# Where the attention starts, where the lists stand and how many expert units are open in a one-core attention and mixture-of-experts block

## The chip, the core and the metric

The kernel runs on one core of a Trainium2 chip, as one program with one launch. The time is device microseconds of that core. Each engine of a core executes its own instructions in order: TensorE (PE in the profile, its weight loads PEld) multiplies, VectorE (DVE), ScalarE (ACT) and GpSimd (POOL) work on elements, and SyncE (SP), ACT and POOL issue transfers. Engines wait for each other through semaphores.

## The reference

The input x is 2 x 1024 x 256. Every row is normalised (mean and variance over 256) to xn, and the output is x + attention(xn) + ffn(xn).

```python
# attention: xn seen as tokens of 16 channels, on a grid of 256 x 64
qkv = tok @ qkv_w                                    # 16 -> 48
x1 = branch(q[:8], k[:8], v[:8], 1 x 8 windows)      # softmax(q k / sqrt(8)) v + 3x3 convolution of v
x2 = branch(q[8:], k[8:], v[8:], 8 x 1 windows)
att = concat(x1, x2) @ proj_w + proj_b
tok = tok + layernorm(att) * ln_w + ln_b
# ffn: 16 experts of 176 hidden units, the best 6 of a row, and one shared expert of 352 units
topk = 6 of the experts in the 2 best of 4 groups, by sigmoid(xn @ gate.T) + bias
out = sum over the 6 of weight * (silu(xn @ g_e.T) * (xn @ u_e.T)) @ d_e.T
out = out + (silu(xn @ sg.T) * (xn @ su.T)) @ sd.T
```

## The kernel before

**Stages.** The kernel normalises the 2048 rows, finds each row's six experts on DVE, and sorts the rows by their set of experts, so that the 16 tiles of 128 sorted rows each have six experts in common for most of their rows. While that is computed, PE works on the shared expert, whose steps `shared_steps` are let in by `meanwhile(until)`. A step `products(k, m)` makes the two products of 512 rows, `gated` multiplies silu of one by the other (ACT L283, DVE L284), and `down` makes the output of 128 rows (PE L290), which ACT writes to `ysum` (L291) and POOL adds to the output in DRAM (L293).

**Units.** Then comes a loop over 55 units of two experts each (L1124). A unit is `six` (two of the six experts of a sorted tile, three units a tile) or `extra` (two lists of 128 rows that have some other expert). Lists are made by `lists_begun` and `lists_ended` while the first units run; the seven extra units stand behind tiles `FIRST` to `FIRST + 6`. Per expert, `up` makes the products for gate and up (PE L867), ACT takes silu (L869, to `sg`), and DVE multiplies (L870, to `hms`): this is called the gating product below. Per unit, `hidden` transposes the two experts' products (PE L881, ACT copy L883), and `finished` makes the output (PE L893 or L901). `hms` has two buffers: `hidden` of unit u - 1 and `finished` of unit u - 2 follow the two `up` of unit u. For an extra unit, POOL gathers rows (L994), PE transposes them (L1001), and ACT copies them (L1003) ahead of `up`. The output of each tile or list goes to `ysum` (L1047, L1054), from which POOL adds it to the output by an indirect DMA (`to_out`, L1008). Two additions to the output are never open at once: each waits until the one before has landed.

**The walk.** The attention is a list of steps, here called the walk (`attention_steps`), that is laid between the units. It has four blocks (batch b, half h of the channels). A block gathers its rows (ACT L670), projects them in eight steps (`project`: PE L675, four ACT copies L677 to L680 each), and then works on DVE alone but for one Exp (ACT L700): products L688, sums L692, maximum and difference L698, L699, weighted values L709, L714, totals L703, L704, division L722. Then PE transposes the result (`transposed`, L729) and ACT copies it to `oT` (L731). Behind the fourth block come the projection of the output and the convolution (`attended`, PE L781) and the normalisation (`normed`, L791 to L806), and eight DMAs that add the attention to the output (L1079).

**Pace.** The walk is paced by a written cost of every step on DVE and on PE: `walked` lets steps in as long as the DVE cost so far is under `pace` times the PE cost so far.

```python
of_slot = {"six": (0.5, 2.0), "extra": (0.8, 2.5)}
END = 84
pace = (whole[0] - LEAD - END * of_slot["six"][0] / of_slot["six"][1]) / (whole[1] - END)
```

`END` is the PE cost that is to be left when the walk ends. The first part of the walk, the gathering and the eight projections of block 0, is let in ahead of the last steps of the shared expert:

```python
sorted_tile(0)
walked(FIRST_ROWS - LEAD)
sorted_tile(1)
meanwhile(100)
walked()
```

**Order.** A scheduler orders the instructions of each engine from the program, so neighbours in the program can change places in the built order.

## Time and profile before

| | |
|---|---|
| median of three runs | 449.19 us (448.36 to 451.4) |
| the profiled execution's own time | 448.94 us |
| its span, first to last instruction | 447.2 us |
| mean granted TensorE clock | 0.978 |
| PE busy | 393.4 us, 88% |
| DVE busy | 293.0 us, 66% |
| ACT busy | 215.6 us, 48% |
| POOL busy | 187.8 us, 42% |
| additions by indirect DMA (L1008) | 30, mean 1701 ns of POOL each |

Busy time is the union of an engine's instructions. The ends of matmuls are modelled, so a PE that is busy throughout is not a PE at its peak. A granted clock of 0.50 is half speed. In the lists of groups and of the timeline a row has line, engine, operation, output and inputs; in brackets stands how long the engine was idle before, and what it waited for.

### The profile page before, as it was taken

The page shows a single profiled execution, that of the slowest core. Times are in us where ns is not written, and L with a number is a line of the kernel's source. Part 1 is how long each engine was busy: PE and PEld are TensorE (multiplying, and loading weights), DVE is VectorE, ACT ScalarE, POOL GpSimd, SP SyncE. Part 2 cuts the span into 40 slices and gives each one's busy share as a digit, 9 for nine tenths or more (in the row PEclk, how much of TensorE's full clock was granted, in tenths as well). Part 3 has the DMA queues.
Part 4 walks back from the last instruction along what each step waited for, and adds up shares of the span by engine and source line. Part 5 has one row for each costly group of instructions (what it writes and reads, how often), then busy time and mean ns, then how long its engine had stood idle before and what let it go on. Part 6 is the DMA issues. An engine that isn't in the chain of part 4 may idle for free. (4 is left out here: it accounts for less than half of the span.)

```text
span 447.2 us, 6291 instructions
## 1 busy us (share of the span) xinstructions
PE 393.4 (88%) x1668; PEld 247.4 (55%) x1669; DVE 293.0 (66%) x515; ACT 215.6 (48%) x535; POOL 187.8 (42%) x207
## 2 busy tenths in 40 slices
PE   0999999997887979898898899999899999999970
PEld 0445565655554646665565476566655555666750
DVE  4627958679997948979779599398992333322110
ACT  2955247462472355372462452735335777843220
POOL 7400000220556145886504235324542778791431
PEclk9999999998999999999999699999999999999995
DMA  8999942320423110121012133202331129347222
GB/s 236 314 290 328 272 170 42 48 82 12 86 70 85 22 20 22 33 38 39 22 24 45 52 60 65 44 20 63 85 58 38 22 65 141 74 70 101 44 33 24
DMA packets 40178, 37.56 MB, mean 84 GB/s; under 512 B 5300, under 2 KB 37616, under 8 KB 40112
## 3 DMA queue, kind: packets, MB, share of 16 engines
q0 software_dynamic: 11616, 13.52, 18.4%
q1 hardware_dynamic: 27472, 22.59, 16.6%
q10 hardware_dynamic: 1056, 1.05, 0.7%
q8 instruction: 15, 0.25, 0.2%
q14 instruction: 19, 0.16, 0.1%
HBM read 27.70 MB, written 12.45 MB: 90 GB/s over the span
## 5 line engine op out<-in xcount | busy, mean ns | idle before, releaser
L867 PE MATMUL pr_u<-w1s,xsT 128*128 x384 | 128.3, 468 | 2.7 <-DVE hms L870 2.1
L867 PEld LDWEIGHTS pr_u<-w1s,xsT 128*128 128x128 f32 x384 | 69.9, 190 | 39.3 <-issue 7.1
L1008 POOL DMA_INDIRECT out_dram<-ysum,lists x30 | 51.0, 1701 | 88.5 <-ACT ysum L1047 38.0
L869 ACT ACTIVATE sg<-pr_u 128x176 f32<-128x176 f32 x110 | 34.6, 317 | 83.1 <-PE pr_u L867 73.6
L870 DVE SCALAR_TENSOR_TENSOR hms<-sg,w,pr_u 128x176 f32<-128x176 f32 x96 | 37.4, 392 | 49.1 <-ACT sg L869 46.6
L688 DVE TENSOR_TENSOR pr<-qk 128x2048 f32<-128x2048 f32 x16 | 36.6, 2288 | 15.8 <-ACT qk L677 15.3
L709 DVE TENSOR_TENSOR pv<-s,v 128x2048 f32<-128x2048 f32 x16 | 36.6, 2286 | 4.2 <-ACT s L700 4.2
L692 DVE TENSOR_REDUCE s<-pr 128x256 f32<-128x2048 f32 x16 | 36.5, 2281 | 0.1
L714 DVE TENSOR_REDUCE o<-pv 128x256 f32<-128x2048 f32 x16 | 36.4, 2272 | 0.0
L293 POOL DMA_DIRECT2D out_dram<-ysum x4 | 3.7, 914 | 76.1 <-ACT ysum L291 76.1
L881 PEld LDWEIGHTS ph<-ident,hms 128*128 128x128 f32 x165 | 21.4, 141 | 19.8 <-issue 8.0
L994 POOL DMA_INDIRECT xg<-xw_d,lists x14 | 21.2, 1512 | 26.2 <-DVE hms L870 23.7
L881 PE MATMUL ph<-ident,hms 128*128 128x128 f32 x165 | 29.5, 276 | 2.2 <-DVE hms L870 1.7
L969 POOL TENSOR_SCALAR ysum<-row_h,spot 128x128 f16<-128x128 f16 x26 | 21.3, 825 | 23.4 <-PE rows_of L960 17.0
L827 POOL DMA_INDIRECT xg<-xw_d,lists x16 | 21.6, 1353 | 18.7 <-PE px__1007 L835 6.5
L893 PE MATMUL pr_y<-w2a,hT 128*128 x96 | 28.7, 380 | 0.0
L893 PE MATMUL pr_y<-w2b,hT 112*128 x96 | 28.7, 379 | 0.0
L893 PE MATMUL pr_y<-wts,hT 128*128 128x256 f32 x96 | 28.5, 379 | 0.0
L290 PE MATMUL py<-room 128*128 128x256 f32 x96 | 25.3, 402 | 2.5 <-DVE room L284 2.5
L883 ACT COPY hT<-ph 128x384 f32<-128x384 f32 x55 | 26.3, 479 | 1.9 <-PE ph L881 1.2
L675 PE MATMUL pq<-wq,rows 128*128 128x384 f32 x64 | 24.8, 503 | 2.5 <-ACT oT L731 1.4
L867 PE MATMUL pr_u<-w1s,xd 128*128 x56 | 21.8, 518 | 5.1 <-ACT xd L1003 4.6
(403 smaller groups left out, 703.6 us busy)
## 6 DMA issues: line engine op xcount, KB each, us to landing
w1s<-in_w_dram SPq DMA_DIRECT2D x22, 256.0 KB
wts<-in_w_dram SPq DMA_DIRECT2D x55, 64.0 KB
wts<-in_w_dram SPq DMA_DIRECT2D x55, 48.0 KB
xw_d<-xx SPq DMA_DIRECT2D x4, 544.0 KB
w2a<-in_w_dram SPq DMA_DIRECT2D x4, 512.0 KB
out_dram<-ysum POOLq DMA_DIRECT2D x4, 512.0 KB, 6.8
xr<-xw_d POOLq DMA_DIRECT2D x4, 512.0 KB
out_dram<-att POOLq DMA_DIRECT2D x8, 256.0 KB, 4.1
```

The costliest lines, as they stand in the source:

```text
L290: nc.tensor.matmul(py, lhsT=hms[k, m][:, P * c : P * c + P], rhs=w2h[:, m], start=(m == 0), stop=(m == 2))
L688: nc.vector.tensor_tensor(pr, q_.unsqueeze(3).to_broadcast(full), k_.unsqueeze(2).to_broadcast(full), ALU.mult)
L692: nc.vector.tensor_reduce(out=s[:, n : n + NW], in_=held.pop(n), axis=AX.X, op=ALU.add)
L709: nc.vector.tensor_tensor(pr, s[:, n : n + NW].unsqueeze(3).to_broadcast(full), v[:, br, m : m + NW].unsqueeze(2).to_broadcast(full), ALU. ...
L714: nc.vector.tensor_reduce(out=o[:, n : n + NW], in_=held.pop(n), axis=AX.X, op=ALU.add)
L867: nc.tensor.matmul(pu, lhsT=lhs[:, h, :], rhs=w1s[:, :, h, bass.ds(e * I, I)], start=(h == 0), stop=(h == 1))
L869: nc.scalar.activation(sg, pu[:, 0, :], AF.Silu)
L870: nc.vector.scalar_tensor_tensor(hm[:, 0:I], sg, w, pu[:, 1, :], op0=ALU.mult, op1=ALU.mult)
L881: nc.tensor.transpose(ph[:, s, :], units[:, P * s : P * s + P], ident)
L883: nc.scalar.copy(hT, ph)
L893: nc.tensor.matmul(py, lhsT=l_, rhs=r_, start=start and n == 0, stop=stop and n == 2)
L1008: nc.gpsimd.indirect_dma_start(out=out_rows, out_offset=bass.IndirectOffsetOnAxis(ap=index, axis=0), in_=ys, in_offset=None, bounds_check= ...
```

## The change

It has four parts.

1. `walked(FIRST_ROWS - LEAD)` is removed: the walk's first steps now follow `meanwhile(100)`, which lets in all that is left of the shared expert.
2. `FIRST` goes from 7 to 8: the first extra unit is unit 27 and not 24, and the last is unit 51 and not 48.
3. `END` goes from 84 to 96, so `pace` from 1.143 to 1.199.
4. From unit `DEEP` = 27 on, three units are open: `hms` has a third buffer (in `ysum`), `hidden` of unit u - 2 follows the first `up` of unit u, and `finished` of unit u - 2 the second; for an extra unit, the second list's `finished` is moved half a unit further. Every fourth `up` from there on takes its PSUM tile from the tag `y1`, so four such tiles are open in place of three. `sg` has three buffers in place of two. To make room, `RING` goes from 4 to 3 (tiles of `ysum` that wait to be added to the output, three for tiles of rows and three for lists), lists use only the PSUM tag `y0`, and some constants of the attention's preparation share a tile of `ysum`.

```diff
-FIRST = 7
-RING = 4
+FIRST = 8
+RING = 3
...
-    hms = work.tile([P, 2, 2, P + HALF], F32, name="hms")
+    hms2 = work.tile([P, 2, 2, P + HALF], F32, name="hms")
+    hms = [hms2[:, 0], hms2[:, 1], ysum[:, 6:8].rearrange("p n d -> p (n d)")[:, 0 : 2 * (P + HALF)].rearrange(
+        "p (e u) -> p e u", e=2)]
...
     def up(hm, lhs, e, w):
-        pu = ps_u.tile([P, 2, I], F32, tag="u", name="pr_u")
+        ups.append(hm)
+        fourth = len(ups) > 48 and len(ups) % 4 == 0
+        pu = (ps_t if fourth else ps_u).tile([P, 2 * I], F32, tag="y1" if fourth else "u", name="pr_u",
+                                             padded_shape=[P, TB]).rearrange("p (a i) -> p a i", a=2)
...
-        sg = work.tile([P, I], F32, tag="sg", name="sg", bufs=2)
+        sg = work.tile([P, I], F32, tag="sg", name="sg", bufs=3)
...
-    def finished(what, hT, wt, e):
+    def finished(what, hT, wt, e, q):
         kind, n, k = what
+        if kind == "six" and q == 0:
+            return
...
         else:
-            for q in range(2):
-                py = sum_tile(1 - q)
-                down_one(py, hT, wt, e[q], q)
-                ys = ysum[:, RING + (n + q) % 4, :]
-                nc.scalar.copy(ys, py)
-                done_.append((ys, lists[:, n + q : n + q + 1]))
+            py = sum_tile(0)
+            down_one(py, hT, wt, e[q], q)
+            ys = ysum[:, RING + (n + q) % RING, :]
+            nc.scalar.copy(ys, py)
+            done_.append((ys, lists[:, n + q : n + q + 1]))
...
-    END = 84
+    END = 96
...
     sorted_tile(0)
-    walked(FIRST_ROWS - LEAD)
     sorted_tile(1)
     meanwhile(100)
     walked()
...
+    DEEP = 3 * FIRST + 3
+
+    def hms_of(u):
+        return hms[u % 2 if u < DEEP else (DEEP % 2, 2, 1 - DEEP % 2)[(u - DEEP) % 3]]
+
-    for u in range(len(laid_out) + 2):
+    for u in range(len(laid_out) + 3):
...
+            if q == 0 and 0 <= u - 3 < len(laid_out) and laid_out[u - 3][0] == "extra":
+                finished(laid_out[u - 3], hT_.pop(u - 3), wts[:, u % 3], begun_.pop(u - 3), 1)
             if u < len(laid_out):
                 if q == 0:
                     fetched(u)
-                begun_.setdefault(u, []).append(begun(laid_out[u], q, hms[:, u % 2]))
-            if q == 1:
-                if 0 <= u - 1 < len(laid_out):
-                    hT_[u - 1] = hidden(hms[:, (u - 1) % 2])
-                if 0 <= u - 2 < len(laid_out):
-                    finished(laid_out[u - 2], hT_.pop(u - 2), wts[:, (u - 2) % 3], begun_.pop(u - 2))
+                if i == 2 * DEEP:
+                    nc.gpsimd.memset(hms[2][:, :, I:], 0.0)
+                begun_.setdefault(u, []).append(begun(laid_out[u], q, hms_of(u)))
+            if u < DEEP:
+                if q == 1 and u >= 1:
+                    hT_[u - 1] = hidden(hms_of(u - 1))
+                if q == 1 and u >= 2:
+                    finished(laid_out[u - 2], hT_.pop(u - 2), wts[:, (u - 2) % 3], begun_.pop(u - 2), 1)
+            elif u - 2 < len(laid_out):
+                if q == 0 and u - 2 not in hT_:
+                    hT_[u - 2] = hidden(hms_of(u - 2))
+                elif q == 1 and laid_out[u - 2][0] == "six":
+                    finished(laid_out[u - 2], hT_.pop(u - 2), wts[:, (u - 2) % 3], begun_.pop(u - 2), 1)
+                elif q == 1:
+                    finished(laid_out[u - 2], hT_[u - 2], wts[:, (u - 2) % 3], begun_[u - 2], 0)
```

More of the change, by code (lines that the diff above doesn't have):

```diff
@@ L97, in numbers @@
         n = pattern[-1][1]
-        ints = pool.tile([P, n], I32, name=name, tag=name if pool is const else "sg", bufs=1 if pool is const else 2,
+        ints = pool.tile([P, n], I32, name=name, tag=name if pool is const else "sg", bufs=1 if pool is const else 3,
                          padded_shape=[P, n] if pool is const else [P, I])
@@ L329, in weights_prepared @@
     def weights_prepared():
+        early = ysum[:, 12]
         qp8 = work.tile([4 * C, 8, C], F32, tag="xd", name="qp8", bufs=2)
@@ L339, in weights_prepared @@
         nc.tensor.transpose(pqp, qp8.rearrange("k t c -> k (t c)"), ident[0 : 4 * C, 0 : 4 * C])
-        qprep = const.tile([P, 4 * C], F32, name="qprep")
+        qprep = early[:, 0 : 4 * C]
         nc.vector.tensor_copy(qprep, pqp)
@@ L359, in weights_prepared @@
                                 band[:, 0, :].unsqueeze(2).to_broadcast([P, 8, C]), ALU.mult)
-        rd = const.tile([C, 5, C], F32, name="rd")
+        rd = early[0:C, 64 : 64 + 5 * C].rearrange("p (a c) -> p a c", c=C)
         nc.vector.tensor_tensor(rd, prep[0:C, :].unsqueeze(1).to_broadcast([C, 5, C]),
@@ L372, in weights_prepared @@
         nc.vector.tensor_tensor(pb, pb, pm[:, 5, :], ALU.add)
-        mm = const.tile([P, 5, C], F32, name="mm")
+        mm = early[:, 144 : 144 + 5 * C].rearrange("p (a c) -> p a c", c=C)
         nc.vector.tensor_copy(mm, pm[:, 0:5, :])
@@ L853, in number @@
                               skip_runtime_bounds_check_because="made from a count below it")
-    hms = work.tile([P, 2, 2, P + HALF], F32, name="hms")
+    hms2 = work.tile([P, 2, 2, P + HALF], F32, name="hms")
+    hms = [hms2[:, 0], hms2[:, 1], ysum[:, 6:8].rearrange("p n d -> p (n d)")[:, 0 : 2 * (P + HALF)].rearrange(
+        "p (e u) -> p e u", e=2)]
     wts = work.tile([P, 3, W], F32, name="wts")
-    nc.gpsimd.memset(hms, 0.0)
-    nc.gpsimd.dma_start(out=xw_d[ROWS : ROWS + 1, :], in_=hms[0:1].rearrange("p a b u -> p (a b u)")[:, 0:ROW])
+    nc.gpsimd.memset(hms2, 0.0)
+    nc.gpsimd.dma_start(out=xw_d[ROWS : ROWS + 1, :], in_=hms2[0:1].rearrange("p a b u -> p (a b u)")[:, 0:ROW])
     nc.gpsimd.memset(wts, 0.0)
+    ups = []
     def up(hm, lhs, e, w):
-        pu = ps_u.tile([P, 2, I], F32, tag="u", name="pr_u")
+        ups.append(hm)
+        fourth = len(ups) > 48 and len(ups) % 4 == 0
+        pu = (ps_t if fourth else ps_u).tile([P, 2 * I], F32, tag="y1" if fourth else "u", name="pr_u",
+                                             padded_shape=[P, TB]).rearrange("p (a i) -> p a i", a=2)
         for h in range(2):
             nc.tensor.matmul(pu, lhsT=lhs[:, h, :], rhs=w1s[:, :, h, bass.ds(e * I, I)], start=(h == 0), stop=(h == 1))
-        sg = work.tile([P, I], F32, tag="sg", name="sg", bufs=2)
+        sg = work.tile([P, I], F32, tag="sg", name="sg", bufs=3)
         nc.scalar.activation(sg, pu[:, 0, :], AF.Silu)
@@ L917, in lists_begun @@
         spot = room_[:, 1024:1280]
-        spoti = [t.bitcast(I32) for t in (room_[:, 1280:1536], ysum[:, 7])]
+        spoti = [t.bitcast(I32) for t in (room_[:, 1280:1536], ysum[:, 5])]
         by_pair = flagged.rearrange("p (e t) -> p e t", t=NTL)
@@ L1084, in csw_block_moe @@
     of_tile = (0.75, 0.25)
-    END = 84
+    END = 96
     in_walk = [4 * (16 * 2.3 + 3.3 + 2.5 + 1.5 + 1.4) + 0.6 + 8 * 1.4, 4 * 6.2 + 8 * 3.9]
-    FIRST_ROWS, LEAD = 2.5, 12
+    LEAD = 12
     done = [float(-LEAD), 0.0]
@@ L1094, in counted, with walked @@
             done[n] += cost[n]
-    def walked(until=None):
+    def walked():
         step = held_.pop()
-        while step and done[0] <= (pace * done[1] if until is None else until):
+        while step and done[0] <= pace * done[1]:
             step[2]()
@@ L1169, in csw_block_moe @@
         middle(wts[:, 0], e__, None)
-        up(hms[:, 0, 0], turned(xg), e, xg[:, bass.ds(e_ + W, 1)])
+        up(hms[0][:, 0], turned(xg), e, xg[:, bass.ds(e_ + W, 1)])
         py = sum_tile(0)
-        down_one(py, hidden(hms[:, 0]), wts[:, 0], e, 0)
+        down_one(py, hidden(hms[0]), wts[:, 0], e, 0)
         ys = work.tile([P, W], F32, tag="xd", name="ys", bufs=2)
```

## The prediction, made before the result was known

> **What bounds the kernel now.** I read the busy table and slices first, then busy time by stretch, then the waits, then the timeline where stages meet.
>
> ```profile
> PE 393.4 (88%) x1668; PEld 247.4 (55%) x1669; DVE 293.0 (66%) x515; ACT 215.6 (48%) x535; POOL 187.8 (42%) x207
> ```
>
> PE looks like the bound, but this is a mean over stages. Busy time by stretch (columns: stretch, length, then busy time of PE, PEld, DVE, ACT, POOL, granted clock, DMA share, GB/s):
>
> ```profile
> 98.42:335.67 237.25, 211.07 (x871) 140.01 (x870) 203.11 (x232) 107.46 (x328) 107.30 (x97) 0.98 0.22 46
> 335.67:433.35 97.68, 95.70 (x378) 60.83 (x376) 26.44 (x58) 55.59 (x101) 57.25 (x48) 1.00 0.39 67
> 433.35:447.20 13.85, 0.00 (x1) 0.00 (x0) 0.00 (x0) 0.37 (x1) 3.09 (x2) 0.67 0.18 20
> ```
>
> There are three stages. From the first product of block 0 (98.42) to the last division (335.67), DVE is busy 203.1 of 237.3 us and idle 34.1; PE is idle too. Behind it PE alone works, 95.7 of 97.7 us. Then 13.9 us pass without PE.
>
> Why is DVE idle in the first stage?
>
> ```profile
> DVE pr L688 <- ACT qk L677: 15.3, 3, 6.8
> DVE pv L709 <- ACT s L700: 4.2, 3, 2.2
> ```
>
> The first row is the passage from one block to the next, three times. The timeline of the third:
>
> ```profile
> 277.97 1.29 DVE L722 TENSOR_TENSOR xo<-o,sums 128x512 f32<-128x512 f32 x2
> 288.10 2.29 DVE L688 TENSOR_TENSOR pr<-qk 128x2048 f32<-128x2048 f32 x1 [6.83 <-ACT qk L677]
> 282.35 1.04 PE L729 MATMUL po<-ident,xo 128*128 128x128 f32 x8
> ```
>
> The division ends at 279.26, yet PE comes to its transposes at 282.35, 3.1 us late, and the next block starts 5.75 us after that. So DVE's chain waits partly for PE being behind. In the timeline the three passages cost DVE 7.4, 5.9 and 7.6 us of idling (20.9); PE is late by 0, 2.4 and 3.1. Exp takes 4.2 and the other waits 9.0, among them 2.65 for the first lists. **The walk is a DVE chain, what follows it a PE chain, and their sum is the time**: less PE work inside the walk saves nothing, and work pushed behind it is paid in full.
>
> **Start behind the shared expert.** Before:
>
> ```profile
> 98.42 2.29 DVE L688 TENSOR_TENSOR pr<-qk 128x2048 f32<-128x2048 f32 x1
> 106.07 1.29 PE L290 MATMUL py<-room 128*128 128x256 f32 x4 [2.52 <-DVE room L284]
> ```
>
> In the built order of the changed kernel all four block rows of the shared expert precede the projections on PE. From 92.0, where both kernels have the same PE work behind them: four transposes 0.5, two pairs of products 3.4 (two pairs from 88.52 to 91.9), twelve output products 5.1 (24 passes at 0.21, L290), four projections 2.6 (0.65 each, L675 at 286.31), ACT's copies 0.6, a short wait for the last gating 0.5. The first product comes at about 104.7; I take 105 (bounds 104.2 and 107), **6.6 us later**, and DVE gets only one small copy more to fill the gap. L284 (0.68) now lies ahead of the chain, and the 2.52 us wait of PE goes; PE is not what counts there. What is moved with it: 32 ACT copies of the projections now stand behind ACT's writes of the shared output, and POOL's last addition for the shared expert (112.89, waited for ACT) can go earlier by some us; POOL's queue behind it holds gathers of tiles that PE does not need for several units, so I cost that at nothing.
>
> **The walk's end.** The program lays the last division six experts sooner; in the built order of DVE it stands behind 76 gating products, before behind 80. So **the change does less than it says**: four experts, not six, since the late start takes two back. The walk's DVE work is thus 203.1 - 4 x 0.39 (L870) - 0.7 = 200.8. Behind the last transposes PE now has 32 experts to begin, before 28, and four extra units, before two. In steady state a unit costs 3.99 us:
>
> ```profile
> 417.18 0.48 ACT L883 COPY hT<-ph 128x384 f32<-128x384 f32 x1
> 421.17 0.48 ACT L883 COPY hT<-ph 128x384 f32<-128x384 f32 x1
> ```
>
> It splits into 1.18 per expert for gate and up, 0.11 per transpose, 0.43 per output product (starts of the rows between). Counting the built order: 4 x 1.18 + 9 x 0.11 + 8 x 0.41 + 8 turned list halves x 0.13 + 0.7 more waits for ACT's copy (0.80 per extra unit now) = **10.7 us more PE work behind the walk**. Also the eight `attended` are packed closer (one expert between two of them, before often a transpose and outputs too), and compete for two PSUM tiles with turned lists: 1.0 us, bounds 0 and 3.
>
> **Three open units, lists later.** The first extra unit now has three units between the end of the lists and its rows; 2.65 us of DVE's waiting goes. PE may be a unit further ahead, so at the second and third passage it should already stand at the transposes. Idle after, worked out: passages (transposes to next product, less gating products done meanwhile) 7.85 - 4 x 0.39 + 0.1 = 6.4, then 5.76 - 3 x 0.39 + 0.1 = 4.7 twice: 15.8. Exp 3 (0 to 4.2; gating products stand in the gap as before), other waits 4.4 (bounds 1 and 9). Sum 23.2 against 34.1: **10.9 us saved**. The extra buffers of `sg` and PSUM add nothing on a DVE chain. `RING` 3: list n waits for the addition of n - 3, one and a half pairs earlier (over 20 us) while an addition takes 4.4 (435.08 to 439.61 below): nothing, up to 4.4 once if POOL is behind. The new memset on POOL (771 ns for the larger one now) lies ahead of the lists. SP's weight loads wait for `finished` of u - 3 and are needed two units (8 us) later: nothing; gathers keep two units of lead.
>
> **The tail.** Before:
>
> ```profile
> 433.39 0.37 ACT L1047 COPY ysum<-pr_y 128x256 f32<-128x256 f32 x1 [2.06 <-PE pr_y L893]
> 435.08 1.54 POOL L1008 DMA_INDIRECT out_dram<-ysum,lists  x1 [1.91 <-DMA out_dram<-ysum,lists]
> 439.61 1.54 POOL L1008 DMA_INDIRECT out_dram<-ysum,lists  x1 [2.99 <-DMA out_dram<-ysum,lists]
> ```
>
> Eight additions queue up behind the attention's DMAs (issued to 402.7), and the last leaves 6.3 us after PE's end. Now these DMAs lie over 40 us before PE's end; ten additions follow, with time to drain. The last two lists leave PE 7.4 us before its end, so the last addition is issued about 1.3 us after it: **5 us saved**. From issue to the end 7.6 us, as before.
>
> **The sum.** Last division 105 + 200.8 + 23.2 = 329.0. Transposes 329.1. PE's end 329.1 + 96.7 (336.64 to 433.35) + 10.7 + 1.0 = 437.5. End 437.5 + 1.3 + 7.6 = 446.4, against 447.2. The execution took 1.74 us more than its span (448.94), so **448.1 us**, against a median of 449.19. About 1% is what a measurement here can tell from no change: 444.7 to 453.7.
>
> **A rule against the change.** DVE now has two runs of 9.0 us without a gating product (weighted, totals, values, reciprocal, weighted). PE can meanwhile fill three tiles (3.5) and finish a unit (1.7), then waits 3.8. The rows:
>
> ```profile
> 103.50:106.10 2.60, 0.08 (x2) 0.03 (x1) 2.60 (x3) 0.00 (x0) 0.00 (x0) 1.00 0.07 28
> 106.10:110.20 4.10, 4.10 (x11) 3.08 (x12) 4.08 (x3) 1.26 (x3) 0.00 (x0) 0.60 0.00 0
> 246.80:253.60 6.80, 5.54 (x11) 2.94 (x12) 2.99 (x4) 2.23 (x4) 1.72 (x2) 0.50 0.17 41
> ```
>
> A wait of 2.5 us, and one of 3.1 before 247, is followed by half clock. The Trainium skill ("TensorE: Matmul & The Clock Gate", "What's actually happening") puts the halving after an idle window of about 3.4 us and the recovery after a busy one. By the rule two dips cost 2 x 1.7 us of PE; by the longer row 2 x 3.4. I charge nothing: between two passages PE needs 20 experts x 2.0 + 8 projections x 0.72 + 1.0 for transposes = 46.8 us, where DVE needs 55 (before, 226.83 to 288.10 with the passage: 61), so 8 us of slack hide either. Without that cover it is 6.8.
>
> **The cases.**
> - Forecast, 45%: 448.1, own range 445 to 453.
> - PE is always ready, 22%: the first passage shrinks like the others (4.3), Exp to 1, the rest to 1. DVE idles 15.7: **440.6**. It decides from idle under 19.8. For it: PE's slack; against: ACT's copies of list numbers stand in the first passage.
> - PE starved by the 9.0 us runs, 25%: at half clock it is late at a passage again, and DVE waits: 448.1 + 6.8 = **454.9**. It decides once DVE idles over 28.8 us. For it: the clock rows; against: the slack.
> - The last two lists and the last tile queue, 8%: one addition more in the tail, 4.4: **452.5**.
>
> Faster 0.22, same 0.47, slower 0.31; range 441 to 456.5, leaving out the lower half of the second case and the upper part of the third.
>
> **To see it right or wrong.** First L689 product near 105; last division near 329; PE's end near 437; last addition under 2 us behind it; DVE idle near 23 in the walk. A division before 325 or after 335 refutes the idle sum; a tail still over 12 us refutes the draining; PE idle for more than 3 us behind the walk refutes the packing.

## The result, and the profile after

The changed kernel takes **463.92 us** (median of 4 runs, 462.43 to 466.44), the kernel before on the same chip 448.77 us (447.72 to 451.4): 1.0334 times as long, 95% interval 1.0267 to 1.0401. It is **slower by about 15 us**, where 448.1 us and a range of 441 to 456.5 us were forecast. The profiled execution took 466.44 us, the longest of the four; its span is 464.7 us.

The busy table of the changed kernel, columns as before (engine, busy time, share of the span, instructions):

```profile
PE 407.1 (88%) x1668; PEld 252.5 (54%) x1669; DVE 290.5 (63%) x515; ACT 215.0 (46%) x535; POOL 188.5 (41%) x208
```

It does not say where the time went: the shares hardly move. The stages do. Busy time by stretch, from the first product L689 to the last division, from there to PE's end, and behind it (stretch, length, busy time of PE, PEld, DVE, ACT, POOL, granted clock, DMA share, GB/s):

```profile
109.11:341.15 232.04, 203.35 (x801) 132.52 (x801) 200.04 (x225) 101.76 (x319) 99.12 (x91) 0.95 0.20 43
341.15:455.62 114.47, 109.60 (x420) 68.09 (x420) 28.00 (x62) 60.04 (x112) 65.75 (x54) 1.00 0.37 64
455.62:464.70 9.08, 0.00 (x0) 0.00 (x0) 0.00 (x0) 0.37 (x1) 1.54 (x1) 0.65 0.13 15
```

| stage, us of the profiled executions | before | forecast | after |
|---|---|---|---|
| first product (L688, now L689) | 98.4 | 105 | 109.1 |
| walk, first product to last division | 237.3 | 224.0 | 232.0 |
| of it DVE busy, DVE idle | 203.1, 34.1 | 200.8, 23.2 | 200.0, 32.0 |
| last division to last transposes' start | 1.0 | 0.1 | 0.1 |
| from there to PE's end | 96.7 | 108.4 | 114.4 |
| PE's end to the last addition's issue | 6.3 | 1.3 | 1.15 |
| from there to the end | 7.6 | 7.6 | 7.9 |

Against before the column sums to +10.7 - 5.2 - 0.9 + 17.7 - 5.1 + 0.3 = 17.5 us, the difference of the two spans, which is 2.5 us more than the difference of the medians. Against the forecast there are three misses: +4.1 ahead of the first product, +8.0 in the walk, +6.0 in PE's work behind it.

**Ahead of the first product.** PE's timeline (start, duration, engine, line, operation, tiles, count; in brackets the idle time before and what it waited for):

```profile
95.70 1.03 PE L290 MATMUL py<-room 128*128 128x256 f32 x4
99.48 6.27 PE L290 MATMUL py<-room 128*128 128x256 f32 x20 [2.76 <-DVE room L284]
```

and DVE's in the same stretch:

```profile
97.05 0.17 DVE L839 COPY wsrt<-xg 128x16 f32<-128x16 f32 x1 [0.35 <-DMA xg<-xw_d,lists]
98.00 0.17 DVE L839 COPY wsrt<-xg 128x16 f32<-128x16 f32 x1 [0.38 <-DMA xg<-xw_d,lists]
...
98.74 0.68 DVE L284 TENSOR_TENSOR room<-room,pu 128x512 f32<-128x512 f32 x1
109.11 2.29 DVE L689 TENSOR_TENSOR pr<-qk 128x2048 f32<-128x2048 f32 x1 [9.68 <-ACT qk L678]
```

PE's last product for the shared expert ends at 95.86. In DVE's order the last gating, L284, stands behind two copies of tile weights (L839) that wait for gathered rows, and it comes at 98.74. PE waits 2.76 us for it, and the granted clock in the stretch behind the wait is 0.56:

```profile
99.50:103.40 3.90, 3.90 (x10) 3.16 (x11) 0.00 (x0) 0.95 (x2) 0.00 (x0) 0.56 0.00 0
```

Before the change such a wait stood beside the walk; now the walk stands behind it.

**In the walk.** The idle time of DVE, taken apart as in the forecast: passages 19.8 us (forecast 15.8), Exp 4.7 (3), the rest 7.5 (4.4). The passages idle 7.9, 6.7 and 5.2 us, where 6.4, 4.7 and 4.7 were forecast. At the first PE is on time (0.45 us behind the division) and the granted clock is 1.00, but ACT is held up. Its timeline there:

```profile
176.41 0.19 ACT L976 COPY spot<-ysum 128x3 f32 x1 [0.83 <-POOL ysum L979]
178.45 0.20 ACT L976 COPY spot<-ysum 128x3 f32 x1 [0.61 <-POOL ysum L979]
178.56 0.26 ACT L678 COPY qk<-pq 128x128 f32<-128x128 f32 x1
```

ACT copies the numbers for the lists (L976) one at a time, each as soon as POOL has made one more pair of one-hot rows (L978, L979: a one at the place that a row takes, zeros elsewhere), which takes POOL 1.02 us; the copies of qk, for which DVE waits, stand between and behind them. From the division to the next product there are eight such copies, in the kernel before seven, and POOL's first pair starts 2.7 us behind the division, before 1.3.

PE's timeline ahead of the second passage:

```profile
209.95 0.25 PE L969 MATMUL rows_of<-ysum 128*128 128x26 f16 x4
211.41 0.17 PE L969 MATMUL rows_of<-ysum 128*128 128x26 f16 x1 [1.22 <-POOL ysum L979]
215.02 0.18 PE L969 MATMUL rows_of<-ysum 128*128 128x26 f16 x1 [3.44 <-POOL ysum L979]
215.51 2.71 PE L876 MATMUL pr_u<-w1s,xsT 128*128 x4 [0.31 <-issue]
...
220.02 0.18 PE L969 MATMUL rows_of<-ysum 128*128 128x26 f16 x1 [1.53 <-POOL ysum L979]
```

Seven list products (L969) are packed between two experts, and three more behind the next one; in the kernel before there was one per expert. In this clump PE waits for POOL's one-hot rows, and at half clock an expert takes 2.71 us. The clock is 0.54 from 212 to 227. The division ends at 231.30, PE's transposes start at 234.64, 3.3 us late, and the passage takes 9.0 us where 5.9 were forecast.

**Behind the walk** PE is idle for 4.9 us of 114.5, and one unit in four is dearer; the experiments take that apart.

### The profile page after: what moved, and what is told of

Same layout as the page of the kernel before. It is cut to its first block, busy times and chain, and to the rows that moved or that the text cites. A ratio compares the mean times of both kernels' runs of the same rounds, so it can differ in the third digit from the quotient of the medians.

```text
span 464.7 us, 6288 instructions
## 1 busy us (share of the span) xinstructions
PE 407.1 (88%) x1668; PEld 252.5 (54%) x1669; DVE 290.5 (63%) x515; ACT 215.0 (46%) x535; POOL 188.5 (41%) x208
## 5 line engine op out<-in xcount | busy, mean ns | idle before, releaser
L876 PE MATMUL pr_u<-w1s,xsT 128*128 x384 | 136.9, 481 | 1.5 <-issue 1.1
L1017 POOL DMA_INDIRECT out_dram<-ysum,lists x30 | 52.0, 1732 | 97.1 <-ACT ysum L1059 42.5
L876 PEld LDWEIGHTS pr_u<-w1s,xsT 128*128 128x128 f32 x384 | 70.9, 197 | 35.4 <-issue 11.5
L879 DVE SCALAR_TENSOR_TENSOR hms<-sg,w,pr_u 128x176 f32<-128x176 f32 x82 | 31.9, 393 | 41.3 <-ACT sg L878 41.1
L689 DVE TENSOR_TENSOR pr<-qk 128x2048 f32<-128x2048 f32 x16 | 36.6, 2288 | 20.1 <-ACT qk L678 14.8
L710 DVE TENSOR_TENSOR pv<-s,v 128x2048 f32<-128x2048 f32 x16 | 36.5, 2280 | 4.7 <-ACT s L701 3.8
L715 DVE TENSOR_REDUCE o<-pv 128x256 f32<-128x2048 f32 x16 | 36.4, 2275 | 0.0
L828 POOL DMA_INDIRECT xg<-xw_d,lists x16 | 21.3, 1330 | 30.1 <-DVE hms L879 9.3
L890 PE MATMUL ph<-ident,hms 128*128 128x128 f32 x138 | 26.8, 283 | 7.4 <-DVE hms L879 4.6
L902 PE MATMUL pr_y<-w2a,hT 128*128 x96 | 30.3, 398 | 2.3 <-ACT hT L892 1.9
L978 POOL TENSOR_SCALAR ysum<-row_h,spot 128x128 f16<-128x128 f16 x26 | 25.7, 1007 | 16.1 <-PE rows_of L969 8.5
L1003 POOL DMA_INDIRECT xg<-xw_d,lists x14 | 20.3, 1448 | 25.5 <-DVE hms L879 12.9
L890 PEld LDWEIGHTS ph<-ident,hms 128*128 128x128 f32 x138 | 18.1, 144 | 21.5 <-DVE hms L879 6.8
L290 PE MATMUL py<-room 128*128 128x256 f32 x96 | 25.6, 409 | 2.8 <-DVE room L284 2.8
L275 PE MATMUL pg<-xnT,room 128*128 128x512 f32 x48 | 24.0, 612 | 0.0
```

Of the source, the lines that this page charges most:

```text
L689: nc.vector.tensor_tensor(pr, q_.unsqueeze(3).to_broadcast(full), k_.unsqueeze(2).to_broadcast(full), ALU.mult)
L710: nc.vector.tensor_tensor(pr, s[:, n : n + NW].unsqueeze(3).to_broadcast(full), v[:, br, m : m + NW].unsqueeze(2).to_broadcast(full), ALU. ...
L715: nc.vector.tensor_reduce(out=o[:, n : n + NW], in_=held.pop(n), axis=AX.X, op=ALU.add)
L876: nc.tensor.matmul(pu, lhsT=lhs[:, h, :], rhs=w1s[:, :, h, bass.ds(e * I, I)], start=(h == 0), stop=(h == 1))
L879: nc.vector.scalar_tensor_tensor(hm[:, 0:I], sg, w, pu[:, 1, :], op0=ALU.mult, op1=ALU.mult)
L890: nc.tensor.transpose(ph[:, s, :], units[:, P * s : P * s + P], ident)
```

## Experiments

Eighteen kernels ran on the chip, in five groups, each with the kernel before on the same chip. The times are ratios to that kernel with their 95% intervals, the stages, in us, those of the profiled execution, which lies up to 3.3 us off the median (for the two-unit kernel of group 3 it took 453.9 us, where the median is 457.2).

**1. The change with the early start put back, with `END` back, and two kernels built up from before.** The edit of the first:

```diff
     sorted_tile(0)
+    walked(FIRST_ROWS - LEAD)
     sorted_tile(1)
     meanwhile(100)
```

The second has only `-END = 96` `+END = 84`. The third is the kernel before with `FIRST` 8, `END` 96 and the late start, two units open; the fourth is the kernel before with the late start alone.

> The changed kernel with its first part alone undone: the gathering and the projections of block 0 lie ahead of the end of the shared expert again. Built order: the last division still stands behind 76 gating products, 33 experts are begun on PE behind the last transposes (32 in the changed kernel), and the clump of seven list products between two experts is gone. Theory A (the late start is paid in full on VectorE's chain, and starts the half-clock stretches): the first product comes at 98 to 99 and not at 109, the last division 10 to 14 us sooner, so 451 to 455 us against 464. Rival B (the start is absorbed, since the pace lets steps in by cost; only the PE work pushed behind the walk is paid): within 3 us of 464.

> The changed kernel with END back at 84. Built order: the last division behind 80 gating products, 27 experts begun behind the last transposes in place of 32, the list clump down to four products. Theory A: the start stays at 109, the walk ends at most 2 us later or some us sooner (less waiting at the clump), and the chain behind it is 10 to 11 us shorter, so 452 to 456. Rival B: 449 to 451, since nothing else was paid. Rival C (three open units make the loop itself slower, in the walk and behind it): over 457.

> The kernel before with parts 1, 2 and 3 of the change (late start, FIRST 8, END 96), but with two open units, RING 4 and two buffers of sg. Built order: VectorE's order is that of the changed kernel, 32 experts behind the last transposes. Theory A: the third open unit does nothing on VectorE's chain and next to nothing behind it, so 461 to 466. Rival C: the third unit costs the 4 to 6 us by which the chain behind the walk was longer than forecast, so 456 to 460. Rival D (the third unit hides waits): over 468.

> The kernel before with the first part alone: the walk starts behind the shared expert. Built order: 80 gating products before the last division, 28 experts behind the last transposes, as before. Theory A: the first product at 109 in place of 98.4, the last division 8 to 11 us later, so 456 to 460 against 449. Rival B: within 3 us of 449.

| kernel | ratio | first product | walk | PE behind it | last addition behind PE's end |
|---|---|---|---|---|---|
| early start | 1.0103 (1.0044 to 1.0162) | 99.1 | 229.2 | 117.7 | 0.7 |
| `END` 84 | 1.0275 (1.0230 to 1.0319) | 106.7 | 235.7 | 102.6 | 3.4 |
| two units | 1.0384 (1.0341 to 1.0428) | 109.4 | 232.5 | 116.1 | 1.9 |
| late start alone | 1.0275 (1.0231 to 1.0319) | 110.0 | 238.9 | 96.7 | 7.6 |

The late start is the largest part: alone it costs 12.7 us of the medians (462.31 against 449.66), and within the change about 2.3% (1.0334 against 1.0103). That it is paid in full on DVE's chain, theory A of both runs, holds: with an early start 455.6 us came, just above the 451 to 455 expected; with the late start alone 462.3 us are even more than the 456 to 460 expected, because the walk and the tail grow by 1.7 and 1.3 us as well. For `END` 84 theory A does not hold: 461.66 us came where 452 to 456 were expected, in the range of rival C (over 457), since what is saved behind the walk (11.8 us) is mostly lost in the walk (3.7), between the division and PE's transposes (3.7) and in the tail (2.3); of the 4.7 us by which its span is shorter, 2.4 are an earlier first product. That was the hint that `END` is close to neutral. With two units 467.26 us came, between theory A (461 to 466) and rival D (over 468). By the ratios the third unit is worth about 2 us here, but the intervals overlap. The traces show what it may be worth: behind the walk PE waits 5.5 us for gathered rows with two units, and 1.15 us with three.

**2. The parts alone, from an early start.** `FIRST` 8 and three units with `END` 84; `END` 96 alone; the same early kernel with `END` 72, away from the change; and the changed kernel with the last gating ahead. The edit of the last (the copies of the first two tiles' weights read, times zero, what the gating writes, so they must follow it):

```diff
+            nc.vector.scalar_tensor_tensor(out=w, in0=hmr[:, 2, 0:16], scalar=0.0, in1=xg[:, W:ROW],
+                                           op0=ALU.mult, op1=ALU.add)
-            nc.vector.tensor_copy(w, xg[:, W:ROW])
```

> The changed kernel with parts 1 and 3 undone: the walk begins ahead of the last shared steps, and END is 84 again; left of the change are three open units and lists a tile later. Theory A (the time is the end of DVE's chain plus PE's work behind it, and the late start and the early end are what cost): the first product is at 98 to 99, the last division at 331 to 335, behind which 28 experts are left, as before; PE works 98 to 103 us on from there, and the last addition follows PE by under 2 us. 444 to 449 us. Rival B (the third unit costs PE time in itself, by single output products between the gate and up products, some 5 us): 452 to 456 us.

> The kernel before with part 3 alone (END 96). Theory A (DVE's chain plus PE's chain): the walk has four gating products fewer and ends 4 to 7 us earlier (at 329 to 332), but PE has 33 experts to begin behind it and not 28, 117 to 119 us and not 96.7: 457 to 461 us. Rival B (an early end costs nothing in itself, since PE's work is only shifted in time, and what is lost behind the walk is gained in it): within 3 us of the kernel before.

> The changed kernel with one thing moved: the last gating of the shared expert (L284) stands ahead of the copies of the first two tiles' weights on DVE, which wait for gathers. Nothing else changes place on PE. Theory A (PE's wait of 2.76 us for L284 and the half clock behind it delay the whole DVE chain): the first product comes 3 to 4 us sooner, at 105 to 106, and the time is 3 to 4 us shorter, 459.5 to 461.5 us on a chip where the changed kernel takes 464. Rival B (the first product is not on the path, or the lost time comes back at the first passage, where PE is late): within 1.5 us of the changed kernel, 462.5 to 465.5 us.

> As the kernel with parts 1 and 3 undone, but END 72, which is away from the change's direction: the last division stands behind 84 gating products and not 80, and PE has 22 to 23 experts to begin behind it and not 28. Theory A (the time is DVE's chain plus PE's chain; a gating product in the walk costs DVE 0.4 us, an expert behind it costs PE 2 us): the walk is 2 to 5 us longer, the last division at 334 to 338; PE's work behind it is 9 to 12 us shorter; the whole 5 to 8 us shorter than with END 84: 438 to 443 us. Rival B (PE is already full in the walk, 211 of 237 us, so that each expert more in the walk delays the blocks by its 2 us): the same time as with END 84, within 2 us.

| kernel | ratio | first product | walk | PE behind it | last addition behind PE's end |
|---|---|---|---|---|---|
| `FIRST` 8, three units, `END` 84 | 0.9999 (0.9976 to 1.0022) | 98.8 | 233.0 | 102.9 | 2.5 |
| `END` 96 alone | 1.0035 (1.0011 to 1.0060) | 98.0 | 232.3 | 108.4 | 0.8 |
| gating first | 1.0275 (1.0232 to 1.0318) | 104.8 | 230.9 | 114.5 | 1.3 |
| `END` 72 | 1.0324 (1.0295 to 1.0352) | 98.1 | 247.8 | 90.4 | 8.2 |

`FIRST` 8 and three units with `END` 84 cost nothing, and 447.5 us lie in theory A's range (444 to 449), though the last addition stands 2.5 us behind PE's end and not under 2. PE's work behind the walk is still 6.2 us longer there than before, with 27 experts left in place of 28 and one extra unit more; the walk and the tail win it back.

`END` 96 alone costs 0.35%: rival B of that run, and A's 457 to 461 us missed. The walk is 5.0 us shorter, the tail 5.5, and PE's work behind 11.7 longer. My 117 us had been read off the kernel with three units, so the difference between 108.4 and 117.7 must lie in parts 2 and 4, or in how they meet part 3.

With the gating first PE runs through, and the first product comes at 104.78; PE's timeline of that kernel has one group for L290 now, without a wait:

```profile
95.83 5.60 PE L290 MATMUL py<-room 128*128 128x256 f32 x24
```

and DVE's:

```profile
104.78 2.29 DVE L689 TENSOR_TENSOR pr<-qk 128x2048 f32<-128x2048 f32 x1 [2.19 <-ACT qk L678]
```

That is 4.3 us sooner. By the ratios the time is 0.6%, about 2.6 us, shorter (1.0275 against 1.0334; the intervals overlap), a little less than theory A's 3 to 4 us. The forecast's 105 was right for the order that it assumed.

`END` 72 is a miss in the other direction: 438 to 443 us were expected, or about those of `END` 84 by rival B, and 462.25 came. The walk is 247.8 us: PE, not DVE, sets it now. The busy row of this walk:

```profile
98.10:345.80 247.70, 220.90 (x894) 146.81 (x893) 204.81 (x236) 108.36 (x329) 112.45 (x98) 0.97 0.21 45
```

and PE's timeline at its end:

```profile
353.45 1.04 PE L730 MATMUL po<-ident,xo 128*128 128x128 f32 x8
```

The last division ends at 345.8, PE's transposes come at 353.45, 7.6 us later, and each passage takes 11.5 to 12.1 us. PE is not full (221 of 248 us), but its order puts some 22 experts ahead of each block's transposes, and that is enough to make it late.

**3. Two units against three, the outputs' order, the lists' place, and an `END` between.** The first is the kernel before with `FIRST` 8 and `END` 96. The second is the changed kernel with an early start in which an extra unit's two lists are finished one right behind the other with a PSUM tile each, as before (no gate and up product uses that tag). The third is the kernel with the gating first and `i >= 16` in place of `i >= 14` for the lists. The fourth is the kernel before with `END = 90`.

> The kernel before with parts 2 and 3 (FIRST 8, END 96), early start, two open units. It stands between the kernel with END 96 alone (1.0035 of before, PE's work behind the walk 108.4 us) and the changed kernel with an early start (1.010 of before, 117.7 us). Theory A (the third unit makes PE's order dearer: output products stand singly, and transposes wait for nothing else to do at the end, 5 us in all; FIRST 8 puts one extra unit more behind the walk, 2.5 us, and its gathers behind the attention's DMAs): PE's work behind the walk is 111 to 113 us, the walk 231 to 233 us, 451 to 454 us in all. Rival B (FIRST 8 is the whole of it, the third unit costs nothing): behind the walk 116 to 118 us, 457 to 460 us. Rival C (all of it is the third unit): behind the walk 108 to 109.5 us, 449 to 450.5 us.

> The changed kernel with an early start and three open units, but the two lists of an extra unit are finished one after the other with a PSUM tile each, as in the kernel before, and no gate and up product takes its tile from that tag. Theory A (in the changed kernel the second list's output products must wait until the only tile is copied out, so they stand singly among the gate and up products, 0.7 us per extra unit): PE's work behind the walk falls from 117.7 to 114 to 115.5 us, the time by 2 to 4 us against the changed kernel with an early start (455.6 us where before takes 449.7). Rival B (the order of the outputs costs nothing; the third unit's cost is waiting for ACT's copies of hT at the end): behind the walk 117 to 118.5 us, within 1.5 us of that time.

> The changed kernel with the last gating ahead (as in the run with that alone, 1.0275 of before), and the lists begun two experts later (from step 16 on and not 14). In the built order the clump of ten list products between experts 33 and 34 becomes four and two, the rest stands behind block 2's projections. Theory A (PE's waits of 1.2, 3.4 and 1.5 us for POOL's spots in that clump and the half clock behind it make PE late at the second passage): these waits shrink to under 2 us in sum, the second passage (9.0 us) becomes 5.5 to 7, and the time is 2 to 4 us shorter, 1.019 to 1.023 of before. Rival B (DVE's chain sets the passage, PE's lateness is hidden): the second passage stays at 8.5 to 9.5 us and the time within 1.5 us, 1.024 to 1.031 of before.

> The kernel before with END 90 alone, between 84 and 96 (1.0035 of before). The three terms of END 96 alone were: walk 5.0 us shorter, PE's work behind it 11.7 longer, last addition 5.5 sooner behind PE's end. Theory A (walk and work behind it move in proportion, the tail's gain comes in full as soon as the attention's DMAs lie a unit earlier): walk 2 to 3 us shorter, PE 5 to 7 longer, the last addition 4 to 5.5 sooner: 0.5 to 2 us faster than before. Rival B (the tail's gain is in proportion too): within 0.7 us of before.

| kernel | ratio | walk | PE behind it | last addition behind PE's end |
|---|---|---|---|---|
| two units, `FIRST` 8, `END` 96 | 1.0186 (1.0163 to 1.0210) | 226.5 | 118.0 | 2.3 |
| two sums | 1.0177 (1.0138 to 1.0216) | 226.7 | 120.3 | 0.7 |
| lists from step 16 | 1.0417 (1.0374 to 1.0459) | 234.2 | 115.8 | 0.7 |
| `END` 90 | 1.0215 (1.0185 to 1.0246) | 233.1 | 115.3 | 0.7 |

Theory A missed in all four, in three by one cause; the first landed in the numbers of its rival B (116 to 118 us behind the walk, 457 to 460 in all), but not by what B named. PE's timeline of the kernel with `END` 90, behind the walk:

```profile
401.63 0.38 PE L1001 MATMUL px__3903<-ident,xg 128*128 128x128 f32 x2
413.36 0.47 PE L1001 MATMUL px__3920<-ident,xg 128*128 128x128 f32 x1 [11.35 <-DMA xg<-xw_d,lists]
413.86 2.71 PE L867 MATMUL pr_u<-w1s,xd 128*128 x4
```

and POOL's:

```profile
401.01 2.05 POOL L806 TENSOR_TENSOR att<-a,xr 128x256 f32<-128x256 f32 x2
403.00 4.73 POOL L1079 DMA_DIRECT2D out_dram<-att  x4
408.04 1.09 POOL L994 DMA_INDIRECT xg<-xw_d,lists  x1 [0.30 <-issue]
```

The rows of the last list are gathered at 408.04, right behind the attention's normalisation and its last four DMAs on POOL; PE waits 11.35 us and runs near half clock until 418. In the two-unit kernel the same wait is 5.6 us, with two sums 4.6, with an early start 2.5, in the changed kernel 1.15, in the kernel before and with `END` 96 alone there is none. So a unit more or less ahead of the end decides whether an extra unit's gathers meet the attention's tail.

The later lists removed the clump's waits for POOL, but then ACT's copies of list numbers wait for POOL one by one (2.93, 0.83, 0.83 and 2.66 us), the copies of hT stand behind them, and PE waits 3.8 and 3.3 us for those. The second passage stayed at 8.9 us, and the block ahead of it took 58.1 us in place of 51.0: the repair failed, and it does not tell A from B. But it bears on the first passage, where no copy of a list number stands in ACT's order any more: that takes 8.4 us in place of 9.5, although PE comes 1.8 us late to it.

**4. The attention's DMAs tied behind the gathers.** In four kernels a DVE instruction on one element of `att` reads the gathered row, so that the last four DMAs follow the gather on POOL:

```diff
+            one = att[m][64 * b : 64 * b + 64, 0, P * n : P * n + 1]
+            nc.vector.scalar_tensor_tensor(one, xg[64 * b : 64 * b + 64, 0:1], 0.0, one, op0=ALU.mult, op1=ALU.add)
```

> The kernel before with FIRST 8 and END 96 (1.0186 of before), and the attention's last four DMAs tied to the gather of list 11, so that on POOL's queue two gathers stand ahead of them and not behind. Theory A (the gather's place on POOL's queue is what PE waits for): PE's wait of 5.6 us for the gathered rows and the half clock behind it go, PE's work behind the walk is 109 to 112 us and not 118, the time 5 to 8 us shorter, 1.001 to 1.008 of before. Rival B (the gather waits for its buffer, not for the DMAs): the wait stays over 3 us, the time within 2 us, 1.014 to 1.023 of before.

> The kernel before with END 90 (1.0215 of before), and the same tie, to the gather of list 13. Theory A: PE's wait of 11.35 us goes with the half clock behind it; PE's work behind the walk is 99 to 102 us and not 115; the last addition 1 to 5 us behind PE's end: 441 to 446 us, 0.985 to 0.996 of before, which would beat both kernels. Rival B (the attention's DMAs, now later, hold the additions up in the tail as in the kernel before): the last addition over 6 us behind PE's end, 446 to 450 us. Rival C (the gather waits for its buffer): within 3 us of the kernel with END 90 alone, 455 to 461 us.

> The changed kernel with an early start (1.010 of before), and the same tie, to the gather of list 11. Theory A: PE's wait of 2.5 us goes; PE's work behind the walk is 114.5 to 116 us and not 117.7, 1.003 to 1.008 of before; what is left above the two-unit kernel with the same tie is the order that the third unit gives PE, 3 to 6 us behind the walk. Rival B (three units cover the gather, and the wait was for something else): within 1 us, 1.008 to 1.013 of before.

> The changed kernel with the same tie and nothing else changed. Theory A: PE's wait of 1.2 us for the gathered rows goes, and no more than that: 1.028 to 1.033 of before, PE's work behind the walk 112.5 to 113.5 us and not 114.4. Rival B (the gathers' place is a large part of the 6 us by which that work exceeds the forecast): 1.018 to 1.026 of before, behind the walk under 111 us.

| kernel with the tie | ratio | without the tie | PE behind the walk, without and with |
|---|---|---|---|
| two units, `FIRST` 8, `END` 96 | 1.0224 (1.0166 to 1.0283) | 1.0186 | 118.0, 120.9 |
| `END` 90 | 1.0216 (1.0170 to 1.0262) | 1.0215 | 115.3, 117.5 |
| the change, early start | 1.0184 (1.0129 to 1.0239) | 1.0103 | 117.7, 121.5 |
| the change | 1.0424 (1.0368 to 1.0481) | 1.0334 | 114.4, 119.8 |

Nothing was gained: theory A missed in all four, and with the tie 1.0224 and 459.4 us came in the first two, in the ranges of the rivals by which the gather waits for its buffer. But the experiment is spoilt by its own tie, and so says nothing for them. DVE of the kernel with `END` 90:

```profile
406.40 0.71 DVE L1082 SCALAR_TENSOR_TENSOR att<-xg,att 64x1 f32<-64x1 f32 x4 [15.19 <-DMA xg<-xw_d,lists]
407.15 1.24 DVE L870 SCALAR_TENSOR_TENSOR hms<-sg,w,pr_u 128x176 f32<-128x176 f32 x3
```

DVE stands idle for 15.19 us until the rows are there, and three gating products (L870), for which PE waits, stand behind it. The wait only changed its place.

**5. A place of their own for the last five lists' rows.** Without any tie: lists 9 to 13 are gathered from unit 33 on, into a part of `ysum` that is free by then, ahead of the normalisation on POOL.

```diff
+            if i >= 66 and 9 + i - 66 < NL:
+                ahead[9 + i - 66] = gathered(lists[:, 9 + i - 66 : 10 + i - 66], i - 66)
...
+        if own is not None:
+            xg = room_[:, ROW * own : ROW * own + ROW]
```

> The kernel before with END 90 (1.0215 of before; PE's work behind the walk 115.3 us, of it 11.35 us waiting for the rows of list 13 and 5.5 us lost to half clock behind that), but the rows of lists 9 to 13 go to a tile of their own and are gathered from unit 33 on, one per half unit, ahead of the attention's normalisation on POOL. PE's order stays. Theory A (the late gather is the whole of it): no wait over 1 us for gathered rows behind the walk, PE's work there 98 to 101 us, the last addition 1 to 5 us behind PE's end: 440 to 446 us, 0.98 to 0.995 of before. Rival B (the additions to the output, which no gather now spaces out, queue up at the end as in the kernel before, 6 us): 445.5 to 450 us. Rival C (PE then waits for something else at the same place): over 452 us.

> The kernel before with FIRST 8 and END 96, two units (1.0186 of before; PE's work behind the walk 118.0 us, of it 5.6 us waiting for gathered rows and about 4 us lost to half clock), with the same own rows for lists 9 to 13. Theory A: PE's work behind the walk 107.5 to 110 us, the walk 226 to 230 us: 442 to 447 us, 0.985 to 0.997 of before; then the third unit's order costs the 5 to 7 us by which the changed kernel's work behind the walk exceeds that (114.4 us, of it 1.2 for gathered rows). Rival B (FIRST 8 costs PE something else): behind the walk over 112 us, 450 us or more.

| kernel with own rows | ratio | without | PE behind the walk, without and with | last addition behind PE's end |
|---|---|---|---|---|
| `END` 90 | 1.0081 (1.0050 to 1.0113) | 1.0215 | 115.3, 102.6 | 7.7 |
| two units, `FIRST` 8, `END` 96 | 1.0103 (1.0073 to 1.0133) | 1.0186 | 118.0, 110.9 | 7.0 |

The wait is gone, PE's work behind the walk falls by 12.7 and 7.1 us, and that the late gather is the cause is thereby shown. (Own rows free the gather of its buffer too; but in the row of 408.04 above it waits for nothing but POOL's own order.) The time falls by half of it only, and misses theory A in both (440 to 446 and 442 to 447 us expected, 453.5 and 453.3 measured): the additions to the output take over, as rival B of the first run had it, though by more than its 445.5 to 450 us. (The number is that of its rival C, over 452 us, but PE waits for nothing else in that place.) POOL of the kernel with `END` 90 and own rows, whose PE ends at 434.6:

```profile
401.58 4.71 POOL L1082 DMA_DIRECT2D out_dram<-att  x4
412.38 1.65 POOL L1011 DMA_INDIRECT out_dram<-ysum,lists  x1 [6.09 <-ACT ysum L1050]
417.01 1.57 POOL L1011 DMA_INDIRECT out_dram<-ysum,lists  x1 [2.98 <-DMA out_dram<-ysum,lists]
...
437.72 1.54 POOL L1011 DMA_INDIRECT out_dram<-ysum,lists  x1 [1.90 <-DMA out_dram<-ysum,lists]
442.29 1.54 POOL L1011 DMA_INDIRECT out_dram<-ysum,lists  x1 [3.03 <-DMA out_dram<-ysum,lists]
```

Eight additions, one each 4.3 us, follow the four DMAs: (442.29 - 412.38) / 7 = 4.27. While they queue, PE's end is not what ends the kernel. No kernel of these beats the kernel before; the nearest are `FIRST` 8 with three units and `END` 84 (0.9999) and `END` 96 alone (1.0035).

## Why the prediction was wrong, point by point

**The frame held.** For this change the walk is a DVE chain and what follows it a PE chain, and DVE's work in the walk was forecast as 200.8 us and measured as 200.0. Three terms were mis-sized (the start by 4.1 us, the walk's idle time by 8.8, PE's work behind it by 6.0), and the sentence on the gathers was wrong.

**The late start: step right, order overlooked.** 6.6 us were forecast, 10.7 measured. The step was "L284 (0.68) now lies ahead of the chain, and the 2.52 us wait of PE goes; PE is not what counts there". The wait did not go; it moved ahead of the chain, where PE does count. With the gating first the product came at 104.8, so 4.3 us are this one place in DVE's order. That the copies ahead of it wait for gathers could be read in the built order of DVE.

**The walk: the idle sum failed.** Measured 32.0 us, forecast 23.2, and the mark set for it (a division after 335) was passed: 341.15, of which 4.1 is the late product. The term "Passages 15.8" measured 19.8, "Exp 3" 4.7, "other waits 4.4" 7.5. The passages before were also misread: the trace has 6.6, 5.9 and 7.7 us of idle time in them (20.3), not 7.4, 5.9 and 7.6, so less could be saved there than it seemed.

From an early start with two units and own rows the same terms are 17.2, 2.6 and 6.0 (walk 227.0 us), from an early start with three units 17.3, 2.9 and 7.6 (229.2). So most of the miss in passages and Exp comes with the late start; the miss in the other waits is there without it too, and its cause stays open. Of the 4.0 us by which the passages missed, 2.0 stand at the second, 1.5 at the first and 0.5 at the third. The rival with PE starved, which decides from 28.8 us of idle time, has its mark passed, but it describes the second passage alone. At the first the rows, and the kernel with later lists, point to ACT's copies for the lists, which the prediction named only against its second case. The rival's own reason, the runs of 9.0 us without a gating product, accounts for one dip: from 135.25 to 145.08 DVE has only block work and tile weights, PE waits 2.77 us for a gating product, and the clock is 0.53 from 147 to 158. The other, 212 to 227, comes with the list clump, which I had not looked for; with an early start the list products stand one per expert again, and the second passage takes 6.9 us. "Three open units" should have kept PE a unit further ahead at the passages; the kernels with two units from an early start have equal or shorter passages (8.5, 6.9 and 5.9 against 8.5, 6.9 and 5.9), so the third unit does nothing there.

**Behind the walk: the order of three units was priced at nothing.** "10.7 us more PE work" and 1.0 for the packing were forecast, 17.7 measured. From run to run it goes from 96.7 to 114.4 in these steps:

| step | us | from |
|---|---|---|
| `END` 96: 32.5 experts left in place of 28, and one extra unit more | +11.7 | 108.4 - 96.7 |
| `FIRST` 8: one extra unit more behind the walk, in place of a unit of sorted rows, and half an expert | +2.5 | 110.9 - 108.4 |
| three units in place of two, no wait for rows in either | +4.3 | (117.7 - 2.5) - 110.9 |
| the late start: 32 experts left in place of 33 | -2.0 | (114.4 - 1.2) - (117.7 - 2.5) |
| waiting for gathered rows | +1.2 | the changed kernel's own 1.15 |
| sum | +17.7 | measured 17.7 |

Each line is the difference of one kernel from the one ahead of it, so the sum comes out by construction. The fourth has a check of its own, half a unit of 3.99 us. The first, second and fourth lines make 12.2, where the prediction had 10.7 for the same things: about right. The missing terms are the third line and the last. Busy time by stretch, PE's work behind the walk with two units and own rows, then with three units and an early start, shows it as PE time and not only as idle time:

```profile
324.70:435.70 111.00, 107.72 (x428) 68.44 (x428) 28.08 (x62) 60.23 (x113) 58.26 (x48) 1.00 0.36 59
328.40:446.10 117.70, 111.38 (x428) 69.66 (x428) 28.02 (x62) 57.65 (x113) 65.50 (x54) 1.00 0.37 62
```

As many matmuls, 428, keep PE busy 3.7 us longer at the same clock. In the changed kernel an extra unit's outputs stand apart:

```profile
424.99 0.59 PE L910 MATMUL pr_y<-w2a,hT 128*128 x2
425.51 0.70 PE L910 MATMUL pr_y<-wts,hT 48*128 48x256 f32 x2
426.14 0.86 PE L876 MATMUL pr_u<-w1s,xsT 128*128 x2
426.93 0.70 PE L910 MATMUL pr_y<-wts,hT 64*128 64x256 f32 x2
```

In the two-unit kernel they are one run:

```profile
390.57 0.60 PE L901 MATMUL pr_y<-w2a,hT 128*128 x2
391.10 0.70 PE L901 MATMUL pr_y<-wts,hT 48*128 48x256 f32 x4
391.73 0.70 PE L901 MATMUL pr_y<-w2b,hT 112*128 x2
```

There four units with one extra unit among them take 18.16 us; in the changed kernel, from 429.01 to 447.94, where no wait for rows falls, 18.93 us. Four such turns, with 0.77 each, make 3.1 us. The rest is the end, where three units are still open and PE has nothing to lay between the transposes and the outputs: two waits of 0.62 us for ACT's copy. That the gaps between matmuls of different kinds are the cause is read from the rows and not shown by an experiment, and the two kernels differ in `RING` and PSUM tags as well; the kernel with a PSUM tile for each list was to show it, but there a wait of 4.6 us for rows covers it.

**The gathers.** "Gathers keep two units of lead" was wrong. In the changed kernel it costs 1.2 us, by luck of the order; in other kernels here up to 11.35 us.

**What was right.** The packing of the eight `attended` cost nothing: from the last transposes' start to the start of the last `attended` product PE needs 45.9 us, before 46.7. The tail fell as forecast, from 6.3 to 1.15 us. That "the change does less than it says" held: the last division stands behind 76 gating products. And "less PE work inside the walk saves nothing" held only in part on this side (with `END` 96 alone the walk has four experts fewer, and DVE idles 3.3 us less in it), and not on the other: with `END` 72, four experts more in the walk made it 14.8 us longer than with 84.

## What to carry to other kernels

When a step is moved ahead of the chain that counts, every wait in that step comes along: look in the built order at what stands ahead of its last instruction on each engine, and what that waits for. A work list that is in order on a slow queue (here gathers behind DMAs on POOL) has to be checked against the new place of everything on that queue, since here the wait jumped from nothing to 11 us with a shift of one unit. And where stages are chained, price the order inside the last one as well as its amount: here as many matmuls, more finely mixed, kept PE busy 3% longer.

## What the hardware showed

**Half clock can follow a wait of about 2 us, and does not always.** In the kernel with an early start PE's waits of 2.14 us (from 135.06, for gathered rows) and 1.91 us (from 217.54, for the division) were each followed by half clock, which fills 3.4 us of each of these stretches:

```profile
138.00:142.00 4.00, 4.00 (x10) 2.36 (x10) 2.73 (x6) 0.70 (x3) 2.38 (x3) 0.57 0.53 85
220.00:224.00 4.00, 4.00 (x12) 2.63 (x11) 1.23 (x3) 2.52 (x6) 0.00 (x0) 0.57 0.00 0
```

In the changed kernel a wait of 2.39 us from 258.95 was followed by none, while the same wait of 2.38 us in the kernel with the gating first, from 253.51, was. All four waits are shorter than the idle window of about 3.4 us in the rule that the prediction cites; from when a wait counts these runs do not show. In all twenty traces, from 95 us to PE's end, each stretch of half clock lasts 3.4, 6.8, 10.2 or 13.7 us.

**POOL stands still beside some of DVE's work.** POOL's one-hot rows for the lists (L978 and L979 of the changed kernel), which the clump waits for, take 0.59 and 0.46 us alone; when one starts beside L710, which multiplies two tensors in SBUF, it ends 0.2 to 0.5 us behind it; DVE's timeline and then POOL's:

```profile
216.76 2.29 DVE L710 TENSOR_TENSOR pv<-s,v 128x2048 f32<-128x2048 f32 x1
```

```profile
216.99 2.53 POOL L978 TENSOR_SCALAR ysum<-row_h,spot 128x128 f16<-128x128 f16 x1
219.95 0.59 POOL L978 TENSOR_SCALAR ysum<-row_h,spot 128x128 f16<-128x128 f16 x1
```

Beside L715, a sum over one tensor (208.76 to 211.03), two of them took 0.59 and 0.60 us. The Trainium skill ("SBUF — State Buffer", "SBUF: two separate sides") describes this: DVE and POOL share a pair of ports, and an operation of DVE with two SBUF inputs holds it to its end against one of POOL that reads SBUF. So list work that is packed beside a block's products waits for them, and beside the sums from 208.76 on it did not.
